# Four chained vision layers on one core: layer 1 and layer 2's gate as stages of their own in the hand-written interleave

## The chip, the cores and the metric

The kernel runs on one core of a Trainium2 chip, with no traffic to other cores. The core has five engines that run side by side, each in its own order: TensorE (PE, matrix products; PEld is its weight load), VectorE (DVE), ScalarE (ACT), GpSimd (POOL) and SyncE (SP, which issues nearly all transfers). The metric is device microseconds (us) of one execution, the median over several.

## The reference

The input x has 16 samples of 64x64 positions and 256 channels, in float32. Four layers are applied, each as x + layer(groupnorm(x)), with 32 groups of 8 channels over all positions of a sample:

```python
x = x + _L0_conv_ref(_gn(x), embeddings)       # nearest of 1024 codes of 256 numbers, by distance
x = x + _L1_conv_ref(_gn(x), Wf, bf, Wg, bg, Wh, bh)
#   f, g (32 wide), h (256 wide) = linear maps; per image row of 64 positions:
#   out = sigmoid(f @ g.T) @ h
x = x + _L2_conv_ref(_gn(x), w1, b1, w2, b2, w3, b3)
#   x0, x1, x2 = one number per position; sm = softmax(x0[i] * x1[m]) over i, 4096 x 4096 per sample
#   gate[m] = sigmoid(sum_i x2[i] * sm[i, m]);  out = gate * x
x = x + _L3_conv_ref(_gn(x), w_qkv, w_out, b_out, gamma, beta)
#   linear attention, 4 heads of 32: q softmax over 32, k softmax over all positions,
#   context = k @ v.T, out = context.T @ q, projected to 256, then a layer norm per position
```

A group norm needs statistics over the whole sample, so within one sample a layer can't start before the one before it has finished. Samples are independent.

## The kernel before

A sample's 4096 positions are cut into 8 chunks of 512 positions (CH = 4 tiles of 128; one chunk is 128 partitions x 2 x 512 floats, channels on partitions, 512 KB). The work of a sample is divided over Python generators:

- `stats0` (L286) reads the input in chunks and makes the statistics of the first norm.
- `stage1` (L302) holds both layer 0 and layer 1. Layer 0, the search, takes four matmuls per tile against the 1024 codes (L376), adds norms and takes the maximum on DVE (L383), finds its index (L388), and POOL adds the chosen code by an indirect transfer to the token tile xc (L389). `back` (L346) transposes xc to channels (L350) into the same chunk tile xt, and DVE takes its statistics (L248). All 8 chunks of the sample stay in the pool `xa` (8 buffers, L52). After the last chunk, `gn_finish` (L250, called at L412) makes scale and mean; the weights of layer 1 are scaled by it. Then `attend` (L431) and `mix` (L475) run per chunk: f and g (L437), h (L448), scores (L465), a sigmoid by tanh (L468, L471), the product (L480), the addition to xt (L484), and a store of the chunk to DRAM (L487).
- `rows2` (L506) reads these chunks and makes the three numbers per position of layer 2; `stage2` (L549), called exps below, makes the softmax: for each half of the positions and each of 32 tiles one exponential of 128x2048 on ACT (L577) and one multiply-and-sum on DVE (L580).
- `stage3` (L604) holds two things. First the gate: per chunk, load (L623), the gate row broadcast to 128 partitions by a transfer (L625), one ACT (L632) and one DVE instruction (L633) per half, statistics, a store (L638). After `gn_finish` at L642, layer 3: first a pass over chunks with keys, values, queries and the context (L666 to L727), then a pass with the output (L744 to L779).

Matmul outputs live in PSUM: `ps_m` has four tiles of one bank (L60), `ps_w` two wide tiles of two banks (L61). The wide ones carry the search's distances pd, and layer 1's ph and po.

The loop at L795 sets the order in which the work is written down. Every generator has a start and a length in slots of one sample, and says at each `yield` how much it has done; the one whose own time is earliest goes next:

```python
        tasks.append((b, 1.0, stage1(b), 263))
        tasks.append((b + 1 + LAGR, 0.1, rows2(b), 8))
        tasks.append((b + 1 + LAG2, 1.0, stage2(b), 160))
        tasks.append((b + 2 + LAG3, 1.0, stage3(b), 170))
```

With a total of 263 and some 160 of it in the search, layer 1 takes the last two fifths of its slot as written. A library then builds each engine's instruction order and all waits from this; a block under `tc.high_priority` comes as if written earlier. A buffer of a pool is given out again when all its users are done. All large transfers are issued by SP, one after another: a transfer that waits for a buffer holds up those behind it.

Of the kernel before, what the change touches and what calls it, by code (L numbers as in the profile page):

```python
# [30 lines left out]
DH = 32  # L31
URGENT = 3000
LAGR = 0.03
LAG2 = 0.2
LAG3 = 0.68


@with_exitstack
def kernel(
# [11 lines left out]
    const = ctx.enter_context(tc.tile_pool(name="const", bufs=1))  # L51
    xa = ctx.enter_context(tc.tile_pool(name="xa", bufs=8))  # L52
    xb = ctx.enter_context(tc.tile_pool(name="xb", bufs=5))
# [130 lines left out]

    gam = s3p.tile([P, C], F32, tag="v2", name="gam", bufs=5)
    nc.scalar.dma_start(out=gam, in_=gamma.rearrange("(o n) -> o n", o=1).to_broadcast([P, C]))
# [55 lines left out]

    def stats_tile(name):
        return small.tile([P, NK, NCHUNK, 6], F32, tag="gn_st", name=name, bufs=3)

# [40 lines left out]
    def stats0(b):  # L286
        tag = f"s0_{b}"
        st = stats_tile(f"st_{tag}")
        src = xT[b].rearrange("(k p) n -> p k n", p=P)
        for ch in range(NCHUNK):  # L290
            xt = xb.tile([P, NK, CW], F32, tag="xb", name=f"xs_{tag}_{ch}")
            nc.sync.dma_start(out=xt, in_=src[:, :, ch * CW : (ch + 1) * CW])
            chunk_stats(st, xt, ch)
            yield 1.5
        with tc.high_priority(offset=URGENT):
            norm0[b] = gn_finish(st, "n0", b)
        yield 2


    x2_d, norm2 = {}, {}  # L300

    def stage1(b):  # L302
# [40 lines left out]

        st1 = stats_tile(f"st1_{tag}")

        def back(ch):  # L346
            for k in range(NK):
# [5 lines left out]
                nc.scalar.copy(xt[ch][:, k, :], pt)  # L353
            chunk_stats(st1, xt[ch], ch)

        load(0)
# [3 lines left out]
        tokens(0)  # L360
        wfg_n = wts.tile([P, NK, 2 * CK], F32, tag="wfg_n", name=f"wfg_{tag}")
        load_wfg(wfg_n)
        wh_n = wts.tile([P, NK, C], F32, tag="wh_n", name=f"wh_{tag}")
        nc.sync.dma_start(out=wh_n, in_=wh.rearrange("(k p) n -> p k n", p=P))
        yield 4
        for ch in range(NCHUNK):
            for t in range(CH):
# [27 lines left out]
                if t == 1:  # L395
                    if ch + 2 < NCHUNK:
                        load(ch + 2)
                    if ch + 1 < NCHUNK:
                        norm(ch + 1)
                        yield 2  # L400
                if t == 2:
                    if ch + 1 < NCHUNK:
                        norm_rows(ch + 1)
                    if ch > 0:
                        back(ch - 1)
                        yield 2
                    if ch + 1 < NCHUNK:
                        tokens(ch + 1)
        back(NCHUNK - 1)
        yield 3  # L410
        with tc.high_priority(offset=URGENT):
            scale, nmean, _ = gn_finish(st1, "n1", b)  # L412

# [14 lines left out]
        hs = {}  # L428
        st2 = stats_tile(f"st2_{tag}")

        def attend(ch):  # L431
# [14 lines left out]
            for t in range(CH):  # L446
# [5 lines left out]
                if t % 2 == 1:  # L452
                    nc.tensor.matmul(
                        ph[:, t - 1 : t + 1, :], lhsT=ones3, rhs=h_row, start=False, stop=True, skip_group_check=True
                    )
            hs[ch] = s1p.tile([P, CH, C], F32, tag="xn", name=f"h_{tag}_{ch}")
            nc.scalar.copy(hs[ch], ph)  # L457
# [17 lines left out]
        def mix(ch):  # L475
# [11 lines left out]
            nc.sync.dma_start(out=d, in_=xt[ch])  # L487
            x2_d[b].append(d)

        attend(0)  # L490
# [111 lines left out]


    def stage3(b):  # L604
        tag = f"s3_{b}"
        dst = out[b].rearrange("(t p) c -> p t c", p=P)
        scale, nmean, _ = norm2.pop(b)
        gd, x2 = gates_d.pop(b), x2_d.pop(b)
        st3 = stats_tile(f"st3_{tag}")
        x3 = []  # L610
        wk_n = wts.tile([P, NK, P], F32, tag="wk_n", name=f"wk_{tag}")
# [3 lines left out]
        nc.sync.dma_start(out=wqv_n[:, :, P:], in_=w_src[:, :, 2, :])  # L615

        xm = small.tile([P, NK], F32, tag="xm", name=f"xm_{tag}")
        nc.gpsimd.tensor_tensor(xm, bet, nmean, ALU.subtract)
        put_row(x_row, xm, by_identity, f"x_{tag}")

        for ch in range(NCHUNK):
            xt = xb.tile([P, NK, CW], F32, tag="xb", name=f"xg_{tag}_{ch}")
            nc.sync.dma_start(out=xt, in_=x2[ch])  # L623
            gb = s3p.tile([P, CW], F32, tag="gb", name=f"gb_{tag}_{ch}")
            nc.sync.dma_start(  # L625
                out=gb,
                in_=gd[ch * CH : (ch + 1) * CH, :].rearrange("t p -> (t p)").rearrange("(o n) -> o n", o=1)
                .to_broadcast([P, CW]),
            )
            u = s3p.tile([P, NK, CW], F32, tag="u4", name=f"u_{tag}_{ch}")  # L630
            for k in range(NK):
                nc.scalar.activation(u[:, k, :], gb, AF.Identity, bias=one, scale=scale[:, k : k + 1])  # L632
                nc.vector.scalar_tensor_tensor(  # L633
                    xt[:, k, :], xt[:, k, :], nmean[:, k : k + 1], u[:, k, :], op0=ALU.add, op1=ALU.mult
                )
            chunk_stats(st3, xt, ch)
            d = dram.tile([P, NK, CW], F32, tag=f"x3_{ch}", name=f"x3_{tag}_{ch}")
            nc.sync.dma_start(out=d, in_=xt)  # L638
            x3.append(d)
            yield 4  # L640
        with tc.high_priority(offset=URGENT):
            scale, nmean, _ = gn_finish(st3, "n3", b)  # L642
            scaled(wk_n, scale, nc.scalar)
# [11 lines left out]
        def queries(ch):  # L655
            qv = qvs.pop(ch)
            pq = bank(f"pq_{tag}_{ch}")
            for t in range(CH):
                nc.tensor.transpose(pq[:, t * P : (t + 1) * P], qv[:, t, 0, :], ident)
            qT = s3p.tile([P, CW], F32, tag="v2", name=f"qT_{tag}_{ch}", bufs=5)  # L660
            nc.scalar.activation(qT, pq, AF.Copy, scale=float(DH ** -0.5))
# [4 lines left out]
        for ch in range(NCHUNK):  # L666
# [8 lines left out]
            if ch > 0:  # L675
                last = nkm[:, ch - 1 : ch]
                nc.gpsimd.tensor_scalar(now, now, last, None, ALU.min)  # L677
                nc.scalar.activation(al[:, ch : ch + 1], last, AF.Exp, scale=-1.0, bias=now)
            kx = s3p.tile([P, CW], F32, tag="v2", name=f"kx_{tag}_{ch}", bufs=5)
            nc.scalar.activation(kx, pk, AF.Exp, bias=now, accum_out=ks[:, ch : ch + 1])  # L680
# [19 lines left out]
            for t in range(CH):  # L700
                nc.tensor.transpose(pkt[:, t * P : (t + 1) * P], kx[:, t * P : (t + 1) * P], ident)
            ek = s3p.tile([P, CH, P], F32, tag="v2", name=f"ek_{tag}_{ch}", bufs=5)
            nc.scalar.copy(ek.rearrange("p t d -> p (t d)"), pkt)
# [40 lines left out]
        for ch in range(NCHUNK):  # L744
# [5 lines left out]
            for pr in range(2):  # L750
# [19 lines left out]
                nc.tensor.matmul(px, lhsT=ones3, rhs=x_row, start=False, stop=True, skip_group_check=True)  # L770
                xs = s3p.tile([P, 2, C], F32, tag="v2", name=f"xs_{tag}_{ch}_{pr}", bufs=5)
                nc.scalar.copy(xs, px)
# [11 lines left out]

    tasks = []
    for b in range(nb):
        if b > 0:
            tasks.append((b - 0.6, 0.3, stats0(b), 14))
        tasks.append((b, 1.0, stage1(b), 263))
        tasks.append((b + 1 + LAGR, 0.1, rows2(b), 8))  # L790
        tasks.append((b + 1 + LAG2, 1.0, stage2(b), 160))
        tasks.append((b + 2 + LAG3, 1.0, stage3(b), 170))
    for _ in stats0(0):
# [45 lines left out]
```

## Time and profile before

| | |
|---|---|
| median of 3 runs | 6173.25 us (6172.92 to 6176.32) |
| the profiled execution | 6179.21 us, span from first to last instruction 6177.5 us |
| PE busy | 5213.1 us, 84% |
| DVE busy | 5135.7 us, 83% |
| ACT busy | 4814.3 us, 78% |
| POOL busy | 2457.9 us, 40% |
| mean granted PE clock | 0.921 of full speed |
| moved by DMA | 924.76 MB, mean 150 GB/s |
| search matmuls (L376) | 1939.2 us of PE |
| exps on DVE (L580) / ACT (L577) | 2388.4 us / 2142.6 us |

Busy is the time in which an engine runs an instruction; two instructions that overlap count once. The page also gives, for each group of equal instructions, the time that its engine stood idle just before them and what released it. A wait for several things is put down to the one that came last. Idle time of an engine that doesn't set the end costs nothing, and a share over the whole span is a mean over stretches with different limits, so the tables of single stretches say more.

### The profile page before, as it was taken

How to read it: one execution, taken by the hardware profiler on the slowest of the kernel's cores; microseconds unless marked ns; L12 is line 12 of the kernel's file. 1: busy time of each engine (PE TensorE's matmuls, PEld its weight loads, DVE VectorE, ACT ScalarE, POOL GpSimd, SP SyncE). 2: the span in 40 equal slices, each digit the busy share in tenths (PEclk: the TensorE clock that was granted, in tenths of full speed). 3: DMA queues.
4: the chain of work that ended last, by engine and by line, in shares of the span. 5: the costliest groups of instructions: out<-in, count | busy, mean ns of one | idle time of the engine just before them, and what ended most of it. 6: DMA issues, size and time to landing. Idle time of an engine off the chain costs nothing. (4 is left out here: it accounts for less than half of the span.)

```text
span 6177.5 us, 72004 instructions
## 1 busy us (share of the span) xinstructions
PE 5213.1 (84%) x23688; PEld 3054.7 (49%) x23688; DVE 5135.7 (83%) x7258; ACT 4814.3 (78%) x7620; POOL 2457.9 (40%) x2147
## 2 busy tenths in 40 slices
PE   8968789798898988989898898989889898886577
PEld 3534354555445554554555445454544545544244
DVE  7489989888798988989888798988879898897953
ACT  4578778888778787878888778888878888787854
POOL 3132334343443435434343443434345343443532
PEclk9989899899999989999899999989999998998788
DMA  5425354456455554555455455554655555443344
GB/s 148 155 51 159 100 173 132 160 148 184 137 141 176 144 178 128 177 167 142 157 146 185 131 149 174 145 172 132 184 157 139 161 147 180 138 129 137 124 148 154
DMA packets 484478, 924.76 MB, mean 150 GB/s; under 512 B 48392, under 2 KB 262280, under 8 KB 475912
## 3 DMA queue, kind: packets, MB, share of 16 engines
q1 hardware_dynamic: 407824, 852.61, 41.7%
q0 software_dynamic: 73728, 67.14, 7.8%
q8 instruction: 188, 3.08, 0.2%
q14 instruction: 186, 1.52, 0.1%
q10 hardware_dynamic: 2552, 0.40, 0.0%
HBM read 684.07 MB, written 235.93 MB: 149 GB/s over the span
## 5 line engine op out<-in xcount | busy, mean ns | idle before, releaser
L580 DVE CUSTOM_DVE_ANT_0 ex_s<-ex_s,x2b_s 128x2048 f32<-128x2048 f32 x1024 | 2388.4, 2338 | 182.4 <-ACT ex_s L577 179.4
L577 ACT ACTIVATE ex_s<-x0b_s,nmax_s,x_r 128x2048 f32<-128x2048 f32 x1024 | 2142.6, 2093 | 256.7 <-DVE num_s L580 201.9
L376 PE MATMUL pd_s<-e,xn_s 128*128 128x512 f32 x4096 | 1939.2, 609 | 48.8 <-DVE m L383 33.2
L389 POOL DMA_INDIRECT xc_s<-in_emb_rows,i_s x512 | 1030.6, 2013 | 990.4 <-DVE i_s L388 528.9
L376 PEld LDWEIGHTS pd_s<-e,xn_s 128*128 128x128 f32 x4096 | 744.7, 194 | 849.4 <-issue 756.2
L383 DVE CUSTOM_DVE_ANT_0 nd_s<-pd_s,nn_s 128x1024 f32<-128x1024 f32 x512 | 619.9, 1211 | 63.8 <-ACT nn_s L371 39.0
L388 DVE FIND_INDEX8 i_s<-m,nd_s 128x8 uint32<-128x1024 f32 x512 | 623.1, 1217 | 0.0
L371 ACT ACTIVATE nn_s<-ne,nx_s 128x1024 f32<-128x1024 f32 x512 | 582.1, 1143 | 7.1 <-DVE i_s L388 5.7
L756 PE MATMUL po_s<-wctx_s,qo_s 128*128 128x512 f32 x1024 | 525.4, 635 | 27.0 <-DVE y_s L775 13.2
L448 PE MATMUL ph_s<-wh_s,xt_s 128*128 128x256 f32 x2048 | 523.2, 397 | 8.8 <-ACT h_s L457 8.6
L693 PE MATMUL pqv_s<-wqv_s,xk_s 128*128 128x256 f32 x2048 | 512.1, 394 | 0.0
L693 PEld LDWEIGHTS pqv_s<-wqv_s,xk_s 128*128 128x128 f32 x2048 | 404.9, 198 | 206.9 <-issue 140.6
L448 PEld LDWEIGHTS ph_s<-wh_s,xt_s 128*128 128x128 f32 x2048 | 388.5, 196 | 166.8 <-issue 66.9
L269 POOL TENSOR_TENSOR s_n<-s_n,mhalf 128x2 f32<-128x2 f32 x64 | 53.6, 838 | 862.4 <-ACT s_n L266 752.2
L760 POOL TENSOR_SCALAR lrs_s<-lss_s 128x2 f32<-128x2 f32 x256 | 161.7, 632 | 541.6 <-ACT po_s L757 541.6
L775 DVE SCALAR_TENSOR_TENSOR y_s<-po_s,lrs_s,xs_s 128x256 f32<-128x256 f32 x512 | 224.3, 473 | 164.8 <-POOL lrs_s L761 137.7
L248 DVE BATCH_NORM_STATS2 st_s<-xt_s 128x6 f32<-128x512 f32 x512 | 329.2, 679 | 18.2 <-ACT xt_s L353 17.3
L757 ACT ACTIVATE po_s<-po_s 128x256 f32<-128x256 f32 x512 | 188.8, 369 | 182.4 <-PE po_s L756 169.2
L756 PEld LDWEIGHTS po_s<-wctx_s,qo_s 128*128 128x128 f32 x1024 | 195.1, 201 | 266.6 <-issue 156.9
L711 POOL TENSOR_TENSOR qv_s<-qv_s,qm_s 128x512 f32<-128x512 f32 x128 | 161.7, 1263 | 371.5 <-DVE qm_s L710 276.0
L480 PE MATMUL po_s<-attn,h_s 128*128 128x128 f32 x2048 | 303.6, 310 | 5.4 <-ACT attn L471 4.3
L480 PEld LDWEIGHTS po_s<-attn,h_s 128*128 128x128 f32 x2048 | 281.6, 220 | 26.7 <-issue 8.7
(190 smaller groups left out, 7952.0 us busy)
## 6 DMA issues: line engine op xcount, KB each, us to landing
xs_s<-in_xT SPq DMA_DIRECT2D x128, 512.0 KB
xt_s<-in_xT SPq DMA_DIRECT2D x128, 512.0 KB
xc_s<-in_x SPq DMA_DIRECT2D x128, 512.0 KB
x_s<-xt_s SPq DMA_DIRECT2D x128, 512.0 KB
xr_r<-x_s SPq DMA_DIRECT2D x128, 512.0 KB
xg_s<-x_s SPq DMA_DIRECT2D x128, 512.0 KB
x_s<-xg_s SPq DMA_DIRECT2D x128, 512.0 KB
xk_s<-x_s SPq DMA_DIRECT2D x128, 512.0 KB
```

Source lines behind the costliest of these rows:

```text
L248: nc.vector.bn_stats(st[:, k, ch, :], xt[:, k, :])
L371: nc.scalar.activation(nn, ne2, AF.Identity, bias=nx2[ch][:, t : t + 1])
L376: nc.tensor.matmul(pd[:, cols], lhsT=xn[ch][:, k, t * P : (t + 1) * P], rhs=e2[:, k, cols], start=(k == 0), stop=(k == NK - 1),)
L383: nc.vector.tensor_tensor_reduce(out=nd, in0=pd, in1=nn, scale=1.0, scalar=-3.0e38, op0=ALU.add, op1=ALU.max, accum_out=m8[:, 0:1],)
L388: nc.vector.max_index(i8, m8, nd)
L389: nc.gpsimd.indirect_dma_start(out=xc[ch][:, t, :], out_offset=None, in_=emb_rows, in_offset=bass.IndirectOffsetOnAxis(ap=i8[:, 0:1], axis=0),
L448: nc.tensor.matmul(ph[:, t, :], lhsT=X[:, k, t * P : (t + 1) * P], rhs=wh_n[:, k, :], start=(t % 2 == 0 and k == 0), stop=False, skip_grou ...
L480: nc.tensor.matmul(po[:, k, t * P : (t + 1) * P], lhsT=hs[ch][:, t, k * P : (k + 1) * P], rhs=at[:, t, :], start=True, stop=True,)
L577: nc.scalar.activation(ex, x0b, AF.Exp, bias=nmax[:, T : T + 1], scale=x01[:, T, 1:2], accum_out=den[:, h, T : T + 1])
L580: nc.vector.tensor_tensor_reduce(out=ex, in0=ex, in1=x2b, scale=1.0, scalar=0.0, op0=ALU.mult, op1=ALU.add, accum_out=num[:, h, T : T + 1],)
L693: nc.tensor.matmul(pqv[:, j, :], lhsT=xt[:, k, t * P : (t + 1) * P], rhs=wqv_n[:, k, :], start=(j == 0 and k == 0), stop=False, skip_group ...
L756: nc.tensor.matmul(po, lhsT=qT[:, t * P : (t + 1) * P], rhs=wctx, start=True, stop=True)
```

## The change

`stage1` is cut in two. It keeps the search, finishes layer 1's norm at its end, and stores every chunk to DRAM from `back`. A new `layer1` reads the chunks again, and does what the second half of `stage1` did. `stage3` is cut in the same way: `gate2` makes the gated chunks and the last norm, `stage3` keeps layer 3. The search's chunk pool has 3 buffers, and layer 1 has a pool of 3 of its own; next loads are issued where a chunk has just been stored. Some small pools change: the gate row has 1 buffer for 2, its product u is made by halves in a tile of its own tag, the tag v2 has 4 buffers for 5, the h tiles no longer share buffers with the search's xn, statistics tiles have one buffer per kind. The tasks get starts that follow from the end of the stage before and from when the same stage is free of the sample before it, with lengths that differ for the last samples.

```diff
-LAG2 = 0.2
-LAG3 = 0.68
+LAG1, LEN1 = 0.06, 0.7
+LAG2 = 0.17
+LAG3, LENG = 0.06, 0.8
+LAG4 = 0.04
...
-    xa = ctx.enter_context(tc.tile_pool(name="xa", bufs=8))
+    xa = ctx.enter_context(tc.tile_pool(name="xa", bufs=3))
+    xm = ctx.enter_context(tc.tile_pool(name="xm", bufs=3))
...
     def stage1(b):
...
         def back(ch):
...
             chunk_stats(st1, xt[ch], ch)
+            d = dram.tile([P, NK, CW], F32, tag=f"x1_{ch}", name=f"x1_{tag}_{ch}")
+            nc.sync.dma_start(out=d, in_=xt.pop(ch))
+            x1_d[b].append(d)
...
                 if t == 1:
-                    if ch + 2 < NCHUNK:
-                        load(ch + 2)
...
                     if ch + 1 < NCHUNK:
                         tokens(ch + 1)
+                    if ch + 2 < NCHUNK:
+                        load(ch + 2)
         back(NCHUNK - 1)
+        with tc.high_priority(offset=URGENT):
+            norm1[b] = gn_finish(st1, "n1", b)
         yield 3
+
+    def layer1(b):
+        tag = f"l1_{b}"
+        scale, nmean, _ = norm1.pop(b)
+        x1 = x1_d.pop(b)
...
+        def load(ch):
+            xt[ch] = xm.tile([P, NK, CW], F32, tag="xm", name=f"xt_{tag}_{ch}")
+            nc.sync.dma_start(out=xt[ch], in_=x1[ch])
+
+        load(0)
+        load(1)
         with tc.high_priority(offset=URGENT):
-            scale, nmean, _ = gn_finish(st1, "n1", b)
...
-            hs[ch] = s1p.tile([P, CH, C], F32, tag="xn", name=f"h_{tag}_{ch}")
+            hs[ch] = s1p.tile([P, CH, C], F32, tag="h", name=f"h_{tag}_{ch}")
...
             nc.sync.dma_start(out=d, in_=xt[ch])
             x2_d[b].append(d)
+            if ch + 2 < NCHUNK:
+                load(ch + 2)
...
+    def gate2(b):
+        scale, nmean, _ = norm2.pop(b)
...
+        for ch in range(NCHUNK):
+            xt = xb.tile([P, NK, CW], F32, tag="xb", name=f"xg_{tag}_{ch}")
+            nc.sync.dma_start(out=xt, in_=x2[ch])
+            gb = s3p.tile([P, CW], F32, tag="gb", name=f"gb_{tag}_{ch}", bufs=1)
...
+            for k in range(NK):
+                u = s3p.tile([P, CW], F32, tag="u2", name=f"u_{tag}_{ch}_{k}")
...
+            nc.sync.dma_start(out=d, in_=xt)
+            x3.append(d)
+            yield 4
+        with tc.high_priority(offset=URGENT):
+            scale, nmean, _ = gn_finish(st3, "n3", b)
+        x3_d[b], norm3[b] = x3, (scale, nmean, xm_)
...
-    tasks = []
+    tasks, free = [], {}
+
+    def task(stage, ready, length, gen, total):
+        start = max(ready, free.get(stage, 0.0))
+        free[stage] = start + length
+        tasks.append((start, length, gen, total))
+        return start + length
+
     for b in range(nb):
+        left = nb - 1 - b
         if b > 0:
-            tasks.append((b - 0.6, 0.3, stats0(b), 14))
-        tasks.append((b, 1.0, stage1(b), 263))
-        tasks.append((b + 1 + LAGR, 0.1, rows2(b), 8))
-        tasks.append((b + 1 + LAG2, 1.0, stage2(b), 160))
-        tasks.append((b + 2 + LAG3, 1.0, stage3(b), 170))
+            tasks.append((b - 0.7, 0.5, stats0(b), 14))
+        task("search", b, 1.0, stage1(b), 160)
+        end = task("layer1", b + 1 + LAG1, LEN1 if left and b else 0.35, layer1(b), 90)
+        task("rows", end + LAGR, 0.1, rows2(b), 8)
+        end = task("exps", end + LAG2, 1.0 if left else 0.6, stage2(b), 160)
+        end = task("gate", end + LAG3, 0.15 if left < 2 else LENG, gate2(b), 36)
+        task("layer3", end + LAG4, (0.5, 0.7)[left] if left < 2 else 1.0, stage3(b), 140)
```

## The prediction

> **What bounds the kernel now.** I began with the page's first part, to see whether one engine is full:
>
> ```profile
> PE 5213.1 (84%) x23688; PEld 3054.7 (49%) x23688; DVE 5135.7 (83%) x7258; ACT 4814.3 (78%) x7620; POOL 2457.9 (40%) x2147
> ```
>
> None is, but three are close. Divided by 16 samples, PE has 326 us, DVE 321 and ACT 301 of work per sample. The first search matmul of one sample stands 368 to 372 us behind that of the last from sample 4 to sample 15, so about 43 us of each such slot is PE idle time. Where in the slot? The table of stretches (start:end and length, then busy us and instructions by engine, granted PE clock, DMA share, GB/s) answers it:
>
> ```profile
> 30.00:171.00 141.00, 130.28 (x467) 61.00 (x468) 101.37 (x174) 69.38 (x94) 50.71 (x35) 0.95 0.49 122
> 231.00:518.00 287.00, 228.43 (x1068) 125.37 (x1066) 232.50 (x310) 215.65 (x290) 73.21 (x47) 0.91 0.38 111
> 2671.00:2896.00 225.00, 205.31 (x844) 111.26 (x843) 198.60 (x295) 182.13 (x273) 106.01 (x87) 0.98 0.49 144
> 2896.00:3039.00 143.00, 114.53 (x636) 77.71 (x635) 121.71 (x158) 117.02 (x205) 48.48 (x47) 0.88 0.57 176
> 5700.00:5900.00 200.00, 104.63 (x314) 55.98 (x313) 169.98 (x198) 160.77 (x244) 97.57 (x65) 0.73 0.40 135
> 5624.00:6177.00 553.00, 368.85 (x1405) 225.67 (x1405) 333.02 (x471) 345.89 (x638) 215.80 (x243) 0.81 0.41 141
> ```
>
> Rows three and four are one slot of the steady part: while search runs, PE is busy 205.3/225 = 91%; from its last chunk through layer 1, 114.5/143 = 80%, with DVE at 85% and ACT at 82%. No engine is full there: that part waits on hand-overs. The last row is the drain: 553 us, of which no engine works 370. The waits name the hand-overs (waiting engine, line, releaser: us, times, longest):
>
> ```profile
> PE psc_s L465 <- ACT fg_s L444: 120.6, 59, 5.4
> PE pt_s L350 <- DMA xc_s<-in_emb_rows,i_s: 103.2, 38, 10.3
> PE pg_n L258 <- DVE mv_n L255: 98.8, 32, 33.1
> PE ph_s L453 <- POOL h_row L141: 45.0, 16, 7.2
> ```
>
> All belong to the end of search, the norm after it, or layer 1. Last, the in-order SP queue:
>
> ```profile
> SPq L311 <- DMA x_s<-xt_s: 345.0, 94, 6.5
> ```
>
> A search load already stands 3.7 us (345.0/94) behind a store that frees its buffer, and no compute wait of weight names that load.
>
> **What the Trainium skill says.** Perfetto Trace Analysis, Optimization Strategy: a kernel whose contended engine changes over time may gain by interleaving its regimes. The 91% and 80% above agree that there are two. Perfetto Trace Analysis, Matmuls: independent matmul groups should rotate through PSUM banks so that eviction overlaps the next group. Two wide tiles do that here; PE's idle time before the search matmuls put down to DVE's eviction is 33.2 us in all. TensorE: Matmul & The Clock Gate, What's actually happening: the clock gate follows recent PE activity. The trace has 0.98 in the 91% stretch, 0.88 in the 80% one, 0.73 in the drain. I add no gain for it in the sum.
>
> **The change, part by part.** Compute is moved, not removed: every compute form is issued as often as before. I cost a stage by adding its groups over 16 and scaling each engine to its busy time, since groups overlap at the edges (PE 0.90, DVE 0.93, ACT 0.94). PE/DVE/ACT us per sample: search 127/86/68, layer 1 69/20/24, rows 8/0/2, exps 0/146/131, gate 0/22/12, layer 3 115/34/54.
>
> *Traffic.* 128 stores and 128 loads of 512 KB come in: 134 MB on 924.76, so about 178 GB/s over a shorter run, against stretches at 144 to 176 now. SP issues 256 more instructions of about 0.36 us (the median of the gate's loads), 92 us on a queue that only waits and issues. Each search load now waits for the store issued just ahead of it, with 3 buffers where there were 8. I price that at 3.7 us, 8 times a slot: 30 us of a blocked SP, behind which stand layer 1's stores and loads and the exps rows. These are wanted about a chunk later (350/8 = 44 us), which hides it. Without that cover all 30 us would reach PE. Lower bound nothing; I take nothing. The single gate-row buffer gives about 35 us between chunks (0.8 of a slot over 8) to cover a load; only the last samples' shortened gates lack this.
>
> *Steady slots.* Layer 1 (0.7 slot) now lies beside the next search (1.0), exps (1.0), gate (0.8) and layer 3 (1.0). The waits of the four rows above get other work in the PE order. In the built order a full slot still has 325/321/301; cut at every search chunk, the busiest engine sums to 344 us. For the old order the same cut gives 356 and took 369, a factor 1.036. PE's 325 at the 91 to 93% of the good stretch gives 349 to 357. Lower bound 326 (PE never idle), upper bound 369 or more. I take 351: 18 us a slot off. If a new stall comes, layer 1's PSUM tiles are late next.
>
> *Fill.* The first five slots hold in the built order (busiest engine over the chunks) 128, 275, 241, 295 and 322 us. The first is search alone, 141 now: 140. The old second slot had 260 and took 287; the third had 303 and took 303. With about 1.035 on the others: 285, 250, 305, 332. The fill is longer because exps of a sample now start 0.9 slots after its search ends, not 0.2 after its layer 1.
>
> *Drain.* After the last search PE has 530, DVE 496 and ACT 520 us left; before it was 453, 425 and 440, which took 658 us, from 5519, where the trace has the last sample's search end, to 6177. DVE's part up to the end of the last exps and gate is 428 (496 less 2 x 34 of layer 3); at the 170/200 = 85% of 5700 to 5900 that is 503. Then layer 3 of samples 14 and 15, which can't both hide: 2 x 115 of PE at 92% is 250. Together 753; I take 750.
>
> *Sum.* 30 before the first search, unchanged, + 140 + 285 + 250 + 305 + 332 + 10 x 351 + 345 for the last search's slot + 750 = 5947 against a span of 6177.5. The profiled run was 6179.2, 1.7 more, and the median of the runs 6173.25, 4 below the span. So 5943, rounded to 5940: 3.8% faster. Of the 230 us, ten slots at 18 and one at 24 give about 204; the rest is fill less drain.
>
> **The rivals.**
>
> *Better mixing (0.15).* PE at 97%, as in the best 40 us pieces, with the clock at 1.00: slots of 335. 11 x 16 = 176 us less, 5765. For it: between 2830 and 2910 PE and DVE were both over 97%. Against: ACT waits on POOL's nkm (277.7 us in all) and layer 3's other chains stay.
>
> *Idle moves instead of going (0.13).* Slots stay at 369, because layer 3's chains (PE waits 197.1 us for kx) now sit beside all else. 5947 + 11 x 18 - 4 = 6141, just faster, from fill and drain alone. For it: DVE is nearly as full as PE, so two engines must both run tight.
>
> *Slower (0.12): wide PSUM tiles.* Search and layer 1 took turns with the two wide tiles; now 32 search tiles and 16 of layer 1 (heads and mixes) share them in one order. An eviction of layer 1 can stand behind an exps instruction: 2.34 us on DVE, 2.09 on ACT. If PE waits 2.3 us at each of 16, it pays 37 us a slot: 5947 + 11 x 37 - 4 = 6350. It decides from (6177 - 5947)/11 = 21 us a slot, 1.3 us for each tile. Against: a wide tile is asked for every 351/48 = 7.3 us, so two allow 14.6, and search at 7 us a tile (225/32) lost almost nothing this way.
>
> **How the numbers follow.** The likeliest, slots between 343 and 362, has 0.6: 5850 to 6065 by itself. Faster is 0.6 + 0.15 and most of the 0.13: 0.85. A measurement here tells 0.2% (12 us) from no change; 0.03 falls within it. Slower is 0.12. The range 5760 to 6160 takes in the third case and half of the second; it leaves out the slower one and the faster half of better mixing.
>
> **What would show it.** Right: first search matmuls about 350 us apart; a stretch of a steady slot with PE near 92% and no 80% part; the waits of fg, pt, mv and h_row on PE well down; about 1059 MB moved; a drain near 750 after the last search. Wrong: idle time before pd, ph or po released by their evictions, tens of us a slot (wide tiles); PE waiting on xm or xa loads (SP); slots still at 369 with larger kx waits. The prediction fails most easily in the drain, sized from a rate of another mix, and in the 351, which assumes that two nearly full engines can stay in step.

## The result: the time hardly moved, and the profile after

The changed kernel takes 6209.47 us (median of four runs, 6206.72 to 6217.63), against 6173.09 us (6169.98 to 6176.32) for the kernel before on the same chip: a ratio of 1.0061, 95% interval 1.0044 to 1.0079. Forecast were 5940 us and a gain of 3.8%; measured is a loss of 0.6%. The profiled execution took 6206.72 us with a span of 6204.7 us, 27.2 more than the 6177.5 of before.

First the page of the changed kernel: busy time of each engine, then what DMA moved.

```profile
PE 5213.1 (84%) x23688; PEld 3030.2 (49%) x23688; DVE 5129.6 (83%) x7258; ACT 4811.9 (78%) x7620; POOL 2435.0 (39%) x2147
...
DMA packets 521345, 1059.02 MB, mean 171 GB/s; under 512 B 52488, under 2 KB 266376, under 8 KB 512776
```

The work is that of before to within one per cent, and the traffic is the 1059 MB that was forecast. PE's busy time is the same, so its idle time grew by the 27 us of the span: it was not removed, it has moved. The stretches of the changed kernel (start:end and length, then busy us and instructions of PE, PEld, DVE, ACT and POOL, granted PE clock, DMA share, GB/s):

```profile
2131.80:2506.50 374.70, 321.90 (x1481) 186.40 (x1481) 320.33 (x453) 299.32 (x477) 155.12 (x133) 0.94 0.56 176
3607.20:3966.50 359.30, 315.83 (x1481) 186.56 (x1480) 318.19 (x451) 298.63 (x476) 154.27 (x133) 0.95 0.58 183
5052.40:5420.00 367.60, 321.18 (x1487) 188.47 (x1487) 317.69 (x449) 306.79 (x485) 165.93 (x133) 0.94 0.56 173
5420.00:6204.00 784.00, 549.42 (x2323) 344.54 (x2321) 495.25 (x682) 523.40 (x956) 270.85 (x333) 0.83 0.42 140
```

The first two rows are two steady slots, from one sample's first search matmul to the next one's. PE is busy 86% and 88% of them: the 91% and 80% parts of before have been mixed into one, at their mean. The third row is the last sample's search, the fourth the drain. With the starts of all 16 searches taken from the two traces, the 27 us are a sum of three terms:

| stretch | before | forecast | after |
|---|---|---|---|
| first five slots | 1532 | 1312 | 1353 |
| the next ten slots | 3693 | 3510 | 3669 |
| from the last sample's first search matmul to the end | 921 | 1095 | 1152 |

(The time ahead of the first search is 31 us in both.) The longer pipeline gains 180 us at the front and gives back 231 at the end. The middle, on which the forecast rested, gave 24 us for 183.

Where did the stalls of the middle go? The waits of the changed kernel (waiting engine, line, releaser: us in all, times, longest), and last the row of the kernel before that belongs to `pkt`:

```profile
PE psc_l L489 <- ACT fg_l L468: 8.5, 6, 4.0
PE pt_s L354 <- DMA xc_s<-in_emb_rows,i_s: 21.1, 8, 4.4
PE pg_n L261 <- DVE mv_n L258: 73.8, 20, 21.6
PE ph_l L477 <- POOL h_row L144: 4.0, 2, 3.4
PE pkt_s L738 <- ACT kx_s L717: 262.0, 76, 12.8
PE pk_s L708 <- DMA xk_s<-x_g: 79.4, 9, 10.7
PE prt_r L567 <- ACT rows_r L561: 68.5, 16, 6.8
PE pd_s L379 <- DVE m L386: 65.8, 47, 6.5
...
SPq L314 <- DMA x_s<-xt_s: 254.0, 95, 7.0
```

```profile
PE pkt_s L701 <- ACT kx_s L680: 197.1, 62, 10.6
```

The first four rows are the hand-overs named in the prediction. They fell from 120.6, 103.2, 98.8 and 45.0 us to 8.5, 21.1, 73.8 and 4.0: 260 us went away, as forecast. In their place stand `pkt`, `pk`, `prt` and `pd`. The first two belong to layer 3's pass over the keys: kx rose from 197.1 to 262.0 us, by 65, and the wait for the key load is new with 79. `prt`, of the exps rows, had 6.1 us before and rose by 62, and `pd`, of the search, rose by 33. The last row of the first list is SP's queue: a search load waits 254.0/95 = 2.7 us for its store, less than the 3.7 assumed.

PE's gaps in a single steady slot, added up from the traces, say the same more finely. Before: 47 us, of which 12.8 stand before `pkt` and most of the rest before layer 1's and the search's hand-overs. After, in the slots of samples 5 to 7, counted from 0: 52 us, 25.6 of it before `pkt`. Samples 9 to 14: 43 us, 12.9 before `pkt`, as much as before, 8.9 before `pk`, 6.5 before `prt`.

### The profile page after: what moved, and what is told of

It reads as the page before. It is cut to its first block, busy times and chain, and to the rows that moved or that the text cites. A ratio compares the mean times of both kernels' runs of the same rounds, so it can differ in the third digit from the quotient of the medians.

```text
span 6204.7 us, 72520 instructions
## 1 busy us (share of the span) xinstructions
PE 5213.1 (84%) x23688; PEld 3030.2 (49%) x23688; DVE 5129.6 (83%) x7258; ACT 4811.9 (78%) x7620; POOL 2435.0 (39%) x2147
## 5 line engine op out<-in xcount | busy, mean ns | idle before, releaser
L379 PE MATMUL pd_s<-e,xn_s 128*128 128x512 f32 x4096 | 1992.8, 621 | 96.0 <-DVE m L386 65.8
L392 POOL DMA_INDIRECT xc_s<-in_emb_rows,i_s x512 | 1117.9, 2183 | 1601.0 <-DVE i_s L391 972.7
L386 DVE CUSTOM_DVE_ANT_0 nd_s<-pd_s,nn_s 128x1024 f32<-128x1024 f32 x512 | 621.0, 1213 | 162.6 <-PE pd_s L379 111.6
L472 PE MATMUL ph_l<-wh_l,xt_l 128*128 128x256 f32 x2048 | 528.9, 396 | 9.6 <-DVE m L386 5.9
L730 PE MATMUL pqv_s<-wqv_s,xk_s 128*128 128x256 f32 x2048 | 493.6, 385 | 2.1 <-ACT attn L492 1.7
L797 POOL TENSOR_SCALAR lrs_s<-lss_s 128x2 f32<-128x2 f32 x256 | 149.2, 583 | 825.6 <-ACT po_s L794 818.5
L472 PEld LDWEIGHTS ph_l<-wh_l,xt_l 128*128 128x128 f32 x2048 | 390.1, 196 | 147.0 <-issue 66.0
L708 PE MATMUL pk_s<-xk_s,wk_s 128*128 128x512 f32 x512 | 293.5, 701 | 79.4 <-DMA xk_s<-x_g 79.4
L738 PE MATMUL pkt_s<-ident,kx_s 128*128 128x128 f32 x512 | 97.8, 322 | 262.6 <-ACT kx_s L717 262.0
L753 POOL TENSOR_TENSOR qv_s<-qv_s,qd_s 128x512 f32<-128x512 f32 x128 | 192.7, 1506 | 298.5 <-DVE qd_s L752 172.7
L748 POOL TENSOR_TENSOR qv_s<-qv_s,qm_s 128x512 f32<-128x512 f32 x128 | 193.5, 1512 | 283.2 <-DVE qm_s L747 224.2
L504 PEld LDWEIGHTS po_l<-attn,h_l 128*128 128x128 f32 x2048 | 256.3, 194 | 54.0 <-issue 41.8
```

Of the source, the lines that this page charges most:

```text
L379: nc.tensor.matmul(pd[:, cols], lhsT=xn[ch][:, k, t * P : (t + 1) * P], rhs=e2[:, k, cols], start=(k == 0), stop=(k == NK - 1),)
L386: nc.vector.tensor_tensor_reduce(out=nd, in0=pd, in1=nn, scale=1.0, scalar=-3.0e38, op0=ALU.add, op1=ALU.max, accum_out=m8[:, 0:1],)
L392: nc.gpsimd.indirect_dma_start(out=xc[ch][:, t, :], out_offset=None, in_=emb_rows, in_offset=bass.IndirectOffsetOnAxis(ap=i8[:, 0:1], axis=0),
L472: nc.tensor.matmul(ph[:, t, :], lhsT=X[:, k, t * P : (t + 1) * P], rhs=wh_n[:, k, :], start=(t % 2 == 0 and k == 0), stop=False, skip_grou ...
L504: nc.tensor.matmul(po[:, k, t * P : (t + 1) * P], lhsT=hs[ch][:, t, k * P : (k + 1) * P], rhs=at[:, t, :], start=True, stop=True,)
L708: nc.tensor.matmul(pk, lhsT=wk_n[:, k, :], rhs=xt[:, k, :], start=(k == 0), stop=(k == NK - 1))
```

## The experiments

The chain that ends at `pkt` runs once per key chunk: PE makes pk (L708), DVE takes its maximum (L711), GpSimd takes the minimum with the last chunk's negated maximum (L714), ACT makes the rescale al (L715) and kx (L717), PE transposes kx (L738). One instruction on 128x1 numbers sits on GpSimd between VectorE and ScalarE. Two explanations stood against each other. **The chain**: the stalls went, and layer 3's key chain, now beside everything else, took their place, paced by its step on GpSimd. **The split itself**: the round trip through DRAM, SP's order, the fewer buffers or the wide PSUM tiles cost what the mixing gained. Below, "the minimum" is L714 (L677 before), and times are medians, each with its ratio to the kernel before measured beside it.

### One part of the change alone (e1, e2, e3)

e1 keeps the new code, round trip and pools, but joins the halves again and gives the tasks the starts and lengths of before. e2 splits only layer 1 off, e3 only the gate.

```diff
+    def joined(*stages):
+        for stage in stages:
+            yield from stage
...
-        task("search", b, 1.0, stage1(b), 160)
-        end = task("layer1", b + 1 + LAG1, LEN1 if left and b else 0.35, layer1(b), 90)
...
+        tasks.append((b, 1.0, joined(stage1(b), layer1(b)), 263))
+        tasks.append((b + 1 + 0.03, 0.1, rows2(b), 8))
+        tasks.append((b + 1 + 0.2, 1.0, stage2(b), 160))
+        tasks.append((b + 2 + 0.68, 1.0, joined(gate2(b), stage3(b)), 170))
```

> The changed kernel's code, with its DRAM round trip of layer 1's chunks and its small buffers, but search and layer 1, and gate and layer 3, run one after the other in one task each, with the starts and lengths of the kernel before. If the round trip, the smaller buffers and the fuller transfer queue cost the gain (theory B), this is slower than the kernel before by 60 us or more (6230 and up), since it pays them and has no interleave. If they are hidden and the new interleave itself does not shorten a slot (theory A, engines coupled by chains), it lies within 30 us of the kernel before: 6175 to 6205.

> Layer 1 is a stage of its own, as in the changed kernel; gate and layer 3 are again one task of one slot. If the two cuts act alike (theory A), it is within 40 us of the changed kernel, 6170 to 6250. If the gate's cut, with its deeper pipeline, is what takes the gain of layer 1's (theory C), it is faster than the kernel before by 60 us or more: 6110 or less.

> The gate is a stage of its own; search and layer 1 are again one task of one slot, with the round trip kept. Theory C the other way round, layer 1's cut being the harmful one: 6110 or less. Theory A: 6170 to 6250, with slots near 369.

Measured: e1 6356.92 us (1.0284, 1.0267 to 1.0302), e2 6611.19 (1.0700, 1.0682 to 1.0718), e3 6604.45 (1.0696, 1.0678 to 1.0714). Two waits of e1:

```profile
PE pt_s L354 <- DMA xc_s<-in_emb_rows,i_s: 221.8, 39, 10.4
PE pfg_l L461 <- DMA xt_l<-x_s: 131.0, 44, 6.7
```

In the old order the new code is dear, 181 us: PE waits 131.0 us for layer 1's loads, which before were no loads at all, and twice as long as before for the gather. So the new code has a price in the old order, and the new order makes up for most of it: 6357 to 6209 is a gain of 147 us from the order. The two half-changes, at slots of 393 to 414 us, fit neither expectation. I have no measured cause for them. They do show that the parts don't add.

### The minimum on VectorE (e4, e5)

The same one-word edit in the changed kernel (e4) and in the kernel before (e5):

```diff
-                nc.gpsimd.tensor_scalar(now, now, last, None, ALU.min)
+                nc.vector.tensor_scalar(now, now, last, None, ALU.min)
```

> The changed kernel with the running minimum of the key pass (one 128x1 instruction per chunk) on VectorE in place of GpSimd, which takes 1.8 us for it and has a queue of its own. TensorE waits 262 us for the key exponentials behind this chain. Theory A, this chain paces the slots: those waits fall by half or more and the time by 80 us or more, to 6130 or less. Theory B, late transfers: under 25 us, 6185 or more, since loads stay late.

> The kernel before with the same single instruction of the key pass on VectorE in place of GpSimd. In the changed kernel this took 205 us off (6209 to 6004). If the POOL queue holds the key chain in the new interleave above all, because search's gathers now stand between all of layer 3's POOL steps, the kernel before gains less than half of it: 6080 to 6160. If it paces both kernels alike, it gains 150 us or more: 6020 or less, and the interleave itself is worth little.

Measured: e4 6004.34 us (0.9723, 0.9706 to 0.9739), 205 below the changed kernel; e5 6079.84 us (0.9846, 0.9830 to 0.9863), 92 below the kernel before. The waits of e4, then the same slot and drain as stretches of e4:

```profile
PE pkt_s L738 <- ACT kx_s L717: 124.4, 50, 16.9
ACT al_s L715 <- DVE nkm_s L714: 29.8, 18, 2.3
```

```profile
3487.20:3833.40 346.20, 311.28 (x1482) 183.68 (x1481) 317.76 (x457) 298.68 (x476) 153.08 (x126) 0.97 0.60 190
5225.00:5999.10 774.10, 546.55 (x2330) 342.64 (x2329) 506.00 (x711) 526.99 (x961) 263.36 (x306) 0.84 0.42 142
```

kx's wait halves, and the wait of ACT for the minimum, 237.5 us in the changed kernel, nearly goes. The ten slots take 3503 us; the prediction had 3510. PE is busy 90% of a slot, and its clock is 0.97 for 0.95, so the same matmuls take 311 us for 316. With the minimum on GpSimd the change costs 0.6%; with it on VectorE it gains 6079.84 to 6004.34, 1.2%. The edit also reorders what the library writes: 4.7% of PE's instructions stand elsewhere. So the 205 us needn't be the chain's; the table in the next part shows that most of the gain isn't.

### Adding to the chain, and taking the step out (e10, e14, e15)

e10 issues the minimum twice, e14 five times (it changes nothing in the numbers), with only 0.2% and 0.3% of PE's order moved. e15 drops it: each chunk takes its own maximum, and the rescale from chunk to chunk makes up for it, so the result is the same.

```diff
                 nc.gpsimd.tensor_scalar(now, now, last, None, ALU.min)
+                nc.gpsimd.tensor_scalar(now, now, last, None, ALU.min)
```

> The changed kernel with the running minimum on GpSimd issued twice, the second one without effect on the value: 112 instructions more on GpSimd, some 60 to 200 us of its 3770 us of idle time. If the key chain through GpSimd paces the slots, each chunk of keys is late by as much again: 100 us or more slower than the changed kernel, 6310 and up. If the gain of 205 us came only from the other instruction order that the edit brings, no change beyond 40 us: 6170 to 6250.

> The changed kernel with the running minimum on GpSimd issued five times, the last four without effect on the value; the instruction order of TensorE stays the same to 0.3%. One repetition cost nothing. If the key chain through GpSimd paces the slots, four repetitions (some 2.4 us more per chunk, 17 us a slot) make it 80 us or more slower than the changed kernel: 6290 and up. If it does not, and the gain of the minimum on VectorE came from the new order, within 30 us: 6180 to 6240.

> The changed kernel without the running minimum: every chunk of keys uses its own maximum, and the context is rescaled from one chunk's to the next's, which gives the same result. The chain is then VectorE to ScalarE with no step on GpSimd, as with the minimum on VectorE (6004), in an order that differs from that one's by some 5% of TensorE's instructions. If the chain is the cause, it is within 30 us of it: 5975 to 6035. If the order is, it may lie anywhere from 6004 to 6210.

Measured: e10 6215.20 us (1.0073, 1.0056 to 1.0090), not to be told from the changed kernel; e14 6451.41 (1.0446, 1.0429 to 1.0464), 242 us slower than it; e15 6024.13 (0.9758, 0.9742 to 0.9775), 185 faster. Waits of e14:

```profile
PE pkt_s L742 <- ACT kx_s L721: 518.8, 109, 20.5
ACT al_s L719 <- POOL nkm_s L718: 486.2, 109, 9.0
```

e14 adds 448 instructions on GpSimd, whose busy time grows by 162.6 us, and none on any other engine, and the kernel is 242 us longer; kx's wait on PE doubles. With PE's order all but fixed, that shows that a longer step in this chain does reach the end. e10 limits it: it lies where the other explanation, the instruction order, had been put. kx's wait on PE is 316.6 us in it, 55 more than in the changed kernel, yet the end doesn't move; what gives these 55 us back I didn't find.

e15 takes the step out, and its order hardly moves: in the traces 0.4% of PE's instructions stand elsewhere than in the changed kernel, 0.7% of VectorE's and 1.6% of ScalarE's, as many as in e14. (In e4 it is 4.9, 6.9 and 9.4%, counted the same way.) So e14 and e15 are a pair: the same order, with the chain longer and shorter.

How long the chain is can be added up from the traces: us per key chunk, mean of the 112 chunks that have a minimum (e15: that had one).

| stretch of the chain | before | changed | e14 | e15 | e4 |
|---|---|---|---|---|---|
| from the end of pk until VectorE starts the maximum | 0.70 | 2.19 | 2.20 | 2.28 | 2.26 |
| the maximum | 0.68 | 0.68 | 0.68 | 0.68 | 0.68 |
| until the minimum starts | 0.92 | 1.41 | 1.44 | | 1.29 |
| the minimum or minima | 1.80 | 1.22 | 4.17 | | 0.20 |
| from there to the end of kx | 1.22 | 1.28 | 0.91 | 1.68 | 2.12 |
| sum: end of pk to end of kx | 5.32 | 6.78 | 9.40 | 4.64 | 6.55 |
| PE's other work between pk and `pkt` | 4.01 | 4.80 | 4.91 | 4.73 | 6.06 |
| PE idle before `pkt` | 1.76 | 2.34 | 4.63 | 0.66 | 1.11 |

In e14 the chain is 2.6 us longer and PE waits 2.3 us more a chunk; in e15 it is 2.1 us shorter and PE waits 1.7 us less; PE's work in between is the same. That is 242 us lost and 185 us gained with the length of the chain. e4 is another matter. Its chain is hardly shorter, 6.55 us for 6.78, because on VectorE the minimum has to wait for its turn too, and kx comes later after it. PE waits less because 25 matmuls for 21 stand between pk and `pkt` in its new order, most of the new ones of the search and of layer 1. So e4's gain goes with its order; which part of it counts no run isolates. In e5 it is alike: a chain of 5.46 us for 5.32, with 4.81 us of PE's work beside it for 4.01.

### Why one 128x1 instruction costs that much

All instances of the minimum, in the changed kernel and then in the kernel before (line, engine, operation, count: shortest/median/longest ns, first to last start):

```profile
L714 POOL TENSOR_SCALAR nkm_s<-nkm_s x112: 270/305/4590, 886.2 to 6145.0; 128x1 f32<-128x1 f32 x112
```

```profile
L677 POOL TENSOR_SCALAR nkm_s<-nkm_s x112: 279/1698/4494, 839.7 to 6116.6; 128x1 f32<-128x1 f32 x112
```

In the changed kernel most take 0.3 us, but some 15 times as long. One of these in the timeline of GpSimd of the changed kernel (start us, us, engine, line, operation, tiles, and in brackets idle time with its releaser), and what VectorE does meanwhile:

```profile
2219.49 1.57 POOL L392 DMA_INDIRECT xc_s<-in_emb_rows,i_s  x1 [9.34 <-DVE i_s L391]
2220.53 3.84 POOL L714 TENSOR_SCALAR nkm_s<-nkm_s 128x1 f32<-128x1 f32 x1
```

```profile
2219.14 0.67 DVE L711 TENSOR_REDUCE nkm_s<-pk_s 128x1 f32<-128x512 f32 x1
...
2219.79 2.28 DVE L606 CUSTOM_DVE_ANT_0 ex_s<-ex_s,x2b_s 128x2048 f32<-128x2048 f32 x1
...
2222.00 2.29 DVE L606 CUSTOM_DVE_ANT_0 ex_s<-ex_s,x2b_s 128x2048 f32<-128x2048 f32 x1
2224.21 0.08 DVE L606 DVE_READ_ACCUMULATOR2_ANT num_s<- 128x1 f32 x1
```

The minimum starts at 2220.53, stands still through two of the exps' multiply-and-sums, and ends at 2224.37, 0.08 us after the second. That is the rule: 36 of the 112 take over 1 us (58 in the kernel before), all 36 end within 0.5 us of the end of such an instruction, and 97% of their time has an exps multiply-and-sum beside it, against 0.4% for those of up to 0.4 us. The Trainium skill (GPSIMD Engine Reference, 1. Specifications) says that GpSimd shares its SBUF interfaces with VectorE, with contention against VectorE instructions that have two SBUF inputs, which the multiply-and-sum has (ex and x2b). The traces agree, and put a size to it: 0.3 us becomes up to 4.6.

The sum of these 112 is 136.6 us after and 202.1 us before, so the slow instances aren't what the change added. Nor is GpSimd's step as a whole. A minimum whose input is ready waits for what is written ahead of it, 1.41 us on average after and 0.92 before; wait and instruction together are 2.63 us after and 2.72 before. ScalarE's waits agree, before and after:

```profile
ACT al_s L678 <- POOL nkm_s L677: 277.7, 83, 9.0
```

```profile
ACT al_s L715 <- POOL nkm_s L714: 237.5, 67, 7.1
```

What the change added is the chain's first stretch, VectorE's turn for the maximum: 2.19 us for 0.70, 245 us for 79 over the 112 chunks. Of the 245 us VectorE spends 96 on exps' multiply-and-sums that stand ahead in its order, for 21 before. So GpSimd's step is the part that can be taken out, but the part that grew is on VectorE, which is 83% busy.

### Traffic, stores and small pools (e6, e8, e9, e12)

e6 stores each search chunk a second time to a tile that nothing reads (67 MB more). e8 lets ACT issue the stores. e9 gives the kernel before the new kernel's small pools (v2 with 4 buffers, one gate row, u by halves). e12 is e9 with e5's edit.

```diff
+            twice = dram.tile([P, NK, CW], F32, tag=f"x1b_{ch}", name=f"x1b_{tag}_{ch}")
+            nc.sync.dma_start(out=twice, in_=xt[ch])
-            nc.sync.dma_start(out=d, in_=xt.pop(ch))
+            nc.scalar.dma_start(out=d, in_=xt.pop(ch))
```

(The first two lines are e6, the last two e8.)

> The changed kernel storing every chunk of layer 1's input twice, the second copy never read: 67 MB and 128 SP instructions more, and the search's next load waits for both. If traffic and the SP queue hold the slots (theory B), 60 us or more slower than the changed kernel: 6270 and up. If loads are early enough (theory A), within 25 us of it: 6185 to 6235.

> The changed kernel with the stores of layer 1's input issued by ScalarE, which has just written them, in place of SP. Theory B, SP's head of line: 40 us or more faster than the changed kernel, 6170 or less. Theory A: within 25 us of it, or slower by what ScalarE's issuing costs (128 x some tenths of a us): 6190 to 6250.

> The kernel before with the changed kernel's small pools only: four v2 buffers for five, one gate-row buffer for two, the gate's product by halves. The changed code under the old order was 181 us slower than the kernel before. If the small pools are most of that, this is slower than the kernel before by 90 us or more: 6265 and up; if the round trip through DRAM and its buffers is, within 40 us: 6160 to 6215.

> The kernel before with the minimum on VectorE and the small pools of the changed kernel, which alone gave 93 and 31 us: the fair partner of the changed kernel with the minimum on VectorE (6004). If the two gains add, 6050; the new interleave with its round trip is then worth 46 us. If both shorten the same wait, 6075 to 6090.

Measured: e6 6217.18 us (1.0070, 1.0050 to 1.0091), the changed kernel's own time within the intervals. In the new order 67 MB and 128 SP instructions more cost nothing that these runs can tell. e8 6283.61 (1.0183, 1.0165 to 1.0201), 74 us slower, which neither expectation had: an issue in ACT's order stands ahead of layer 3's ACT steps, as I read it, and PE waits longer for kx:

```profile
PE pkt_s L738 <- ACT kx_s L717: 308.3, 79, 21.6
```

e9 6140.52 (0.9948, 0.9929 to 0.9967): the smaller pools don't hurt the old kernel, they help it by some 31 us, more than either expectation allowed. PE's wait for fg is 70.7 us in it for 120.6, and that for qv_row 41.8 for 77.6; why fewer buffers do that I didn't measure. e12 6058.57 (0.9807, 0.9788 to 0.9825). It is the fair partner of e4, since both have the small pools and the minimum on VectorE: the split and its order are then worth 6058.57 to 6004.34, 54 us or 0.9%.

### Layer 3 later (e11, e13)

If layer 3 started a tenth of a slot later after the gate, its loads would be older when used. e11 is e4 with LAG4 at 0.14 for 0.04; e13 also moves the first step of layer 3's last norm (L797) to VectorE.

```diff
-LAG4 = 0.04
+LAG4 = 0.14
...
-                nc.gpsimd.tensor_scalar(rs, ss, 1.0 / C, 1e-3, ALU.mult, ALU.add)
+                nc.vector.tensor_scalar(rs, ss, 1.0 / C, 1e-3, ALU.mult, ALU.add)
```

> The changed kernel with the minimum on VectorE, and layer 3 starting 0.14 of a slot after the gate's end in place of 0.04, so that its second key load is not queued on SP behind the exps' gate store, which waits for the end of a sample's exps. TensorE waits some 8.5 us a slot there. If that wait costs its length, 50 to 90 us faster than the 6004 without it: 5915 to 5955. If another wait takes its place, within 25 us of 6004.

> As the run with layer 3 later, and the layer norm's scaling of the sum (128x2, 256 times) on VectorE too, so that one of GpSimd's two steps there is gone. VectorE waits 152 us for these in the changed kernel. If GpSimd's queue is still the pace, 30 us or more faster than that run; if VectorE, now near full, is, the same or slower by up to 30.

Measured: e11 6146.53 us (0.9955, 0.9938 to 0.9972), 142 us worse than e4; e13 6263.95 (1.0142, 1.0123 to 1.0161), worse again by 117; no expectation had either. Two waits of e11:

```profile
PE pqv_s L734 <- POOL qv_row L144: 201.8, 16, 20.8
PE pk_s L708 <- DMA xk_s<-x_g: 115.6, 13, 10.8
```

The load's wait is still there, and another GpSimd product, the bias row of queries and values, comes up to 20.8 us late for each sample: 201.8 us for 24.0 in the changed kernel. That a shift of a tenth of a slot meets other neighbours in GpSimd's queue, and that the step of e13 now waits in VectorE's order for ACT, with search and exps behind it, is how I read these losses; no run isolates them.

### The rows of layer 3's norm (e16 to e19)

Ahead of the queries' bias row, GpSimd made another row of the same buffers, `x_row`, which is needed only in the last pass: ACT waited 99.7 us for it. The change had put it there: in the kernel before it was made ahead of the gate's chunks. e16 (on e15), e17 (on the changed kernel) and e18 (on e4) move it behind the fourth key chunk. e19 is e16 with the store of the gate row issued by ACT, to see whether that store, which waits in SP's queue for the exps' end, is what makes the key load late.

```diff
-        put_row(x_row, xm_, by_identity, f"x_{tag}")
...
+            if ch == 3:
+                put_row(x_row, xm_, by_identity, f"x_{tag}")
```

> As the run without the minimum, and the row of layer 3's residual, which the change put directly ahead of the row of queries and values, is made after the fourth chunk of keys. Both rows take about 10 us of GpSimd each, and ScalarE waits 6.7 us a slot for the first. If that wait counts, 40 us or more faster than the run without the minimum alone; if it is covered, within 25 us of it.

> The changed kernel with this row made after the fourth chunk of keys, and nothing else; the instruction order of TensorE stays the same to 0.6%. If the moved row holds the start of layer 3, 40 us or more faster than the changed kernel: 6170 or less. If the key chain is the pace and not the row, within 25 us: 6185 to 6235.

> The changed kernel with both edits that gained: the minimum on VectorE (6004 alone) and the residual's row after the fourth chunk of keys (31 us in the changed kernel, 35 us without the minimum). If they add, 5965 to 5980; if the row only shows where the chain has other orders, 5995 to 6015.

> The run without the minimum and with the row later (5989), and the one small store of the gate per sample issued by ScalarE. On SP this store waits for the end of a sample's exps, and layer 3's second key load stands behind it, for which TensorE waits some 9 to 12 us a slot. If this head of line on SP costs its length, 5880 to 5930; if loads of the exps rows, which wait for the same exps, hold SP in its place, within 25 us of 5989.

Measured: e16 5989.05 us (0.9706, 0.9690 to 0.9722), 35 below e15; e17 6178.01 (1.0006, 0.9997 to 1.0015, twelve runs), 31 below the changed kernel; e18 5965.34 (0.9661, 0.9645 to 0.9677), 39 below e4 and the fastest of all; e19 5973.73 (0.9671, 0.9655 to 0.9687), 15 below e16. The row is worth 31 to 39 us with or without the minimum on GpSimd, and adds to the other gain. So 31 of the 36 us that the change lost go with the place that it gave this row: with only the row moved it ties with the kernel before. (The gains of e16 and e17 lie between the two cases that were expected of each.) With the row moved too, e18 against e12, the split is worth 93 us for the 54 above. One wait of the changed kernel that e17 doesn't have, then waits of e16 and of SP's queue in it, then waits of e19:

```profile
PE pt_s L354 <- ACT row_qv_s L137: 22.7, 4, 5.8
```

```profile
PE pkt_s L736 <- ACT kx_s L715: 60.8, 32, 9.2
PE pk_s L707 <- DMA xk_s<-x_g: 97.4, 10, 14.2
...
SPq L625 <- DVE qd_s L750: 172.1, 8, 22.9
SPq L625 <- DVE grow_s L623: 79.1, 8, 15.6
```

```profile
PE pkt_s L736 <- ACT kx_s L715: 202.6, 33, 17.6
...
PE pk_s L707 <- DMA xk_s<-x_g: 4.0, 4, 1.6
```

In e16 SP stands 251 us at L625, the gate row's store, until DVE has made the row at the end of exps, and the load of a key chunk stands behind it. (In half of the cases the profile names qd, a neighbour of the row in DVE's order. In the changed kernel it is 128.2 and 87.0 us.) With the store on ACT the load's wait is gone, 4.0 us for 97.4, which points to that store, though 2.5% of PE's instructions stand elsewhere too. Of these 93 us the kernel keeps 15. kx's wait rises instead, 202.6 us for 60.8, and 127 of the 203 us stand at one place: before the second key chunk of samples 5 to 12. One such place in the timelines of PE and of VectorE in e19:

```profile
2752.25 1.12 PE L736 MATMUL pkt_s<-ident,kx_s 128*128 128x128 f32 x4 [17.36 <-ACT kx_s L715]
```

```profile
2749.63 0.74 DVE L654 SCALAR_TENSOR_TENSOR xg_g<-xg_g,nm_n,u_g 128x512 f32<-128x512 f32 x1
2750.30 0.68 DVE L710 TENSOR_REDUCE nkm_s<-pk_s 128x1 f32<-128x512 f32 x1
```

PE had finished pk by 2731. VectorE takes its maximum at 2750.30, just behind the first gate instruction (L654). From 2734.33 on it had no idle time: it ran exps and search instructions that stand ahead of the maximum in its order. Once the load is early, the maximum is late by its place on VectorE, the same stretch that grew with the change.

## Why the prediction was wrong

The step that failed is "Steady slots", at "I take 351": ten slots took 3669 us for 3510, so 159 of the 258 us by which the sum fell short. The first half of that step held: the waits of the four rows did get other work in PE's order, and fell by 260 us. The second half failed, that PE would then be busy 91 to 93%: PE was busy 87% of the ten slots, with 46 us of idle time a slot for the 26 that 325 in 351 leaves. It put new waits at nothing. The old search stretch that it took as the measure was itself held by the key chain: of the 20 us of PE idle time in it, 12.5 stood before `pkt`, and in ten slots of the old kernel all of this wait, 128 us, fell beside search. In the new slot the chain is longer, 6.78 us a chunk for 5.32, by VectorE's turn. Of the 46 us, 17.2 stand before `pkt` (12.8 before the change), 6.3 before `pk` and 4.6 before `prt` (both near 0 before), 3.7 before `pd` (0.8). (The row's 31 us, of e17, aren't in these slots: its ten take 3669 us too.)

That is the rival "Idle moves instead of going", put at 0.13, with the wait that it named: slots of 359 to 376 for its 369, kx at 262.0 us. But kx is only 65 us of what rose; the key load and the exps rows rose by as much each, and it named neither. Its sum, 6141, was too low because it left fill and drain as forecast.

Each engine's busy time was in the working, but no chain across engines was priced, though the rows of before showed one: ACT's wait for nkm, 277.7 us, was quoted as a reason against better mixing only. Neither GpSimd at 40% nor the turn on VectorE was weighed as a pace. e14 and e15 show, with the order all but fixed, that this chain's length reaches the end: the ten slots take 3854 and 3530 us for 3669. The key load's and the rows' waits are in e15 as they were. e4's 3503 us lie near the forecast, but by another sum, and so in part by luck: a slot of 350 with PE busy 314 and idle 37, for 325 and 26.

The other steps:

- **Traffic**, taken as nothing: right for the new order (e6), at 2.7 us a load for 3.7. In the old order the new code costs 181 us (e1), with 131.0 us of PE's wait for layer 1's loads in it. So the cover that the step named is needed.
- **Fill**: 1353 for 1312. The five slots took 135, 256, 280, 336 and 346 for 140, 285, 250, 305 and 332. Of the 41 us too many, the first three slots together hold -4, and the fourth and fifth, where exps and layer 3 enter, 45. In e4 these two take 329 and 339, so about a third goes with e4's edit.
- **Last slot and drain**: 368 for 345, and 784 for 750. The drain's estimate from another mix's rate was good to 4.5%. e4 has 774.
- **Slower: wide PSUM tiles**: PE's idle time before the search matmuls that DVE's eviction released rose from 33.2 to 65.8 us in all, 2 us a sample more for the 37 of that rival. It was right that the kernel would be slower, but not for this reason.
- **Better mixing**: its clock did not come by itself (0.94 and 0.95 in the slots), and came in part when stalls went: 0.97 in e4, with PE busy 5134.0 us for 5213.1. Both agree with the statement of the Trainium skill that the prediction cited, on a clock that follows recent activity (TensorE: Matmul & The Clock Gate, What's actually happening). That a kernel with two regimes may gain by interleaving them (Perfetto Trace Analysis, Optimization Strategy) holds here only with other edits: 54 us between e12 and e4, none without them.

Open are the half-changes e2 and e3, why e9's smaller pools help, why one more minimum (e10) costs nothing at the end, and what in e4's order brings its 205 us.

## What to carry to other kernels

Before interleaving stages to fill an engine, write down each stage's chain across engines and price at each step the wait for a turn in that engine's order, on the nearly full engine and on the least busy one: here 2.19 us on VectorE and 1.41 us on GpSimd, for instructions of 0.7 and 0.3 us. Then ask how much of the first engine's own work stands beside the chain. Two things went with a shorter wait: a step less in the chain (e15), and, in e4, more independent matmuls between its two ends. Moving the tiny instruction off GpSimd made it fast, 0.20 us for 1.22, but not the chain, since it waited for its turn on VectorE instead. When code is cut into stages, look at what else moves with the cut: one small row put into the wrong place cost 31 us. To learn whether a step paces a kernel, repeat it several times or take it out, with the order fixed, and check the order in the traces; one repetition may be too few.

## What was not expected of the hardware

A 128x1 GpSimd instruction takes 0.27 us or up to 4.59 us, by what VectorE runs at the time: with two exps instructions of 2.28 us back to back beside it, it took 3.84 and ended with the second. And with shorter stalls the matmuls themselves were faster: with PE busy 90% of a slot (e4) for 88% (changed kernel) the granted clock was 0.97 for 0.95, and PE's busy time in that slot 311.28 us for 315.83, with one instruction more in 1482.
